# A planned one-core graph kernel: fewer early sums, one batch fewer kept on chip, one more left for the last stage, and both ends rearranged

## The chip, the core and the metric

The kernel runs as one program on one core of one Trainium2 chip. The metric is the device time of one execution in microseconds (us), lower is better. The core has a matrix engine (PE in the profile, its weight loads PEld), a vector engine (DVE), a scalar engine (ACT), a general engine (POOL) and a queue engine (SP) that issues most transfers. Engines run beside each other, each takes its own instructions in their written order, and they wait for each other through semaphores. A result of the PE goes to one of eight banks of PSUM and is read from there by ACT or DVE.

## The reference

There are 32 graphs ("batches") of 512 nodes with 128 features, `x` of (32, 512, 128), and a symmetric 0/1 adjacency `adj` of (32, 512, 512). Four layers follow each other, each of them a residual on a normalised input. Cut to what is computed:

```python
def layer0(x, mask, Wv, bv, Wk, bk, Wq, bq):          # masked attention
    v, q, k = (relu(x @ W.T + b) for W, b in ((Wv, bv), (Wq, bq), (Wk, bk)))
    s = q @ k.T
    h = clip(s * mask, 0, 9e13) - 9e15 * (1 - mask)
    return softmax(h, axis=2) @ v

def layer1(x, A, conv_w, conv_b, w_ih, w_hh, b_ih, b_hh):
    A_norm = d_inv[:, :, None] * (A + I) * d_inv[:, None, :]      # d: row sums of A + I
    dyn = conv1d(x[:, -128:, :], conv_w, padding=1) + conv_b      # the last 128 nodes
    lw = lstm(dyn, w_ih, w_hh, b_ih, b_hh)                        # 128 steps, all 32 batches side by side
    return sigmoid((A_norm @ x) @ lw)

def layer2(nodes, A, params):                          # four sublayers, fed by skips
    for i in range(4):
        src = l2norm(A, 2) @ (nodes @ ws + bs)
        dst = l2norm(A, 1).T @ (nodes @ wd + bd)
        nodes = tanh(concat(src, nodes @ wn + bn, dst) @ wu + bu)
    return nodes

def layer3(x, A, W, bias, a):
    g = A @ (x @ W.T) + bias
    return where(g >= 0, g, a * g)

for layer in (layer0, layer1, layer2, layer3):
    x = x + layer(relu(layernorm(x)), adj)
```

## The kernel before, in words

The function `symmetric` is what runs; `general` is a fallback that is entered only when a flag, computed from the data, says so. In its last lines every engine loads that flag (`counted`, `read`) and branches on it, so the branch is the last thing of each engine.

**Recorded, then planned.** The kernel's helpers (`PE`, `ACT`, `DVE`, `POOL`, `DMA`) don't emit instructions. They record operations with an assumed duration, a rank and the buffers they read and write. `Plan.run` then sets all of them in time by a list schedule with those assumed durations, and emits each engine's instructions in the order of the planned starts. So a constant that only the planner reads (`SWITCH`, `HOLD`, `LANDED`, `STORED`, `PATIENCE`, `LEAD`, `FIRST_GAPS`) costs nothing by itself on the chip, and yet can reorder all engines. `SWITCH` is what the planner assumes for the PE's change between whole-array and quarter-array matmuls; `LANDED` and `STORED` are how long after its issue a transfer is assumed to be complete; `PATIENCE` is by how much a long operation may run over the moment at which the LSTM's next operation is expected.

**Four stages.** `pass_1` takes a batch's keys, values and last 128 nodes through layer 0, far enough for the LSTM's input. It stores keys, hidden features and values to DRAM (`f_dkq`, `f_dv`), except for the batches in `RESIDENT`, which come last in pass 1 and keep theirs on chip. `lstm` then runs the 128 steps, each a chain PE `f_z` (line 1303), ACT `f_th` (1329), DVE `f_cu` and `f_th` (1335, 1336), ACT `f_tcn` (1343), DVE `f_h` and the turned copy into `f_seq` (1348, 1349), which the next step's `f_z` needs as its weights. Beside it, `pass_2` computes the other 384 nodes of layer 0: `f_pq` (1399), four score blocks `f_s` (1409), and `f_po` (1415), all quarter-array matmuls. Their order between two LSTM steps is the planner's. `rest` then does layers 1 to 3 of a batch.

**Which batch does what where.** For batches in `EARLY` (0 to 23) pass 2 also computes layer 1's sums beside the LSTM (`f_pg`, eight whole-array matmuls through `aggregate`, line 1538), stores them (`f_dgT`) and `rest` loads them again. The next two (`NEXT`, 24 and 25) and two more (`FIRST`, 26 and 27) go first through `rest`; `FIRST` keep their adjacency on chip from pass 2. The last `LATE` batches (28 to 31) have the lowest priority in pass 2, load only 384 columns of the adjacency there, and compute their sums in `rest`.

**The ends.** At the start ACT's queue loads the attention weights, the column biases and a row bias (`load_beside`), then ACT loads its function table; SP loads `x` and `adj` of the first batches; the PE runs 20 `warm_up` matmuls on zeros until the first `x` is normalised. At the end the last batch is split into two halves; 16 more warm-ups fill the PE's waits; DVE's `f_x` (1709), ACT's `f_neg` (1713) and DVE's `f_x` (1714) form the result of each half, which SP and ACT store. The recorded order of the flag's load is "after the last stores' issue".

Of the kernel before, what the change touches and what calls it, by code (L numbers as in the profile page):

```python
# [521 lines left out]
class Plan:  # L522
# [11 lines left out]
    SLACK = {"PE": 0.25, "ACT": 0.05, "DVE": 0.05, "POOL": 0.05, "SP": 0.05}  # L534


    SWITCH = (0.28, 0.1)
    HOLD = 0.15
    AHEAD = 264
    FETCH = 4.8  # L540
# [72 lines left out]
    def run(self, tc, queues):  # L613
# [15 lines left out]
        for o in ops:  # L629
            if o.rank >= self.last:  # L630
                k, sub = divmod(o.rank - self.last, 10)
                if sub == 2:
                    apart.add(o)
                soon = self.soon if k < 2 and sub < 2 else 0.0
                first = self.lead if sub == 4 else 0.0
                o.rank = self.last - soon + 12 * k - 9 * max(0, k - 28) + 200.0 - first - (min(behind[o], 60) if sub == 5 else behind[o] + (70 if sub == 2 else 0.0))
        self.left = sum(o.rank < self.URGENT for o in ops)
        free = {}
# [155 lines left out]
def symmetric(ctx, tc, x, adj, weights, cols, rows, lstm_b, prelu_a, out, fail):  # L794
# [16 lines left out]
    L = NT - 1  # L811
    NR = N - P
    MANY = 512 // (4 * B)
    LATE = 4
    FIRST = [B - LATE - 2 + k for k in range(2)]
    EARLY = range(24)
    NEXT = [len(EARLY), len(EARLY) + 1]
    FOLD_AT = (2, 3, 4, 5)
    SD_AT = 65
    BOUNCED = 8  # L820
    Q_FIRST = range(0)
    RESIDENT = range(3)
    FIRST_GAPS = (2.0, 2.8, 3.0, 3.5)
    LEAD = 0.0
    Q_AT = 3
    MOVED = range(2, B - 2)
    TURN = 32
    T_STEP = 0.22
    SOON = 9_950.0
    LANDED = 3.3  # L830
    STORED = 3.0
    PATIENCE = 1.3
    plan_rest = 30_000
    assert D == P and N == 512

# [14 lines left out]
    def flat(ap):  # L850
        return ap.rearrange("p a b -> p (a b)")
# [26 lines left out]
    def t_dve(n):  # L878
        return 0.145 + n * 0.00088
# [7 lines left out]
    def ACT(rank, t, fn, r=(), w=(), **k):  # L887
        return plan.op({"ACT": (t, fn)}, rank, r, w, **k)

    def DVE(rank, t, fn, r=(), w=(), **k):  # L890
        return plan.op({"DVE": (t, fn)}, rank, r, w, **k)
# [4 lines left out]
    def DMA(rank, kb, fn, r=(), w=(), **k):  # L896
        return plan.op({"SP": (max(0.45, t_dma(kb)), fn)}, rank, r, w, gap=k.pop("gap", 2.0), **k)
# [6 lines left out]
    def evict(rank, n, dst, src, r, w, relu=False, scale=None):  # L904

        def act():
            nc.scalar.activation(dst(), src(), AF.Relu if relu else AF.Copy, **({} if scale is None else {"scale": scale}))

        def dve():
            if relu:  # L910
                nc.vector.tensor_scalar_max(dst(), src(), 0.0)
            elif scale is not None:
                nc.vector.tensor_scalar_mul(dst(), src(), scale)
            else:
                nc.vector.tensor_copy(dst(), src())

        slow = 0.0 if scale is None else 0.2
        return plan.op({"ACT": (t_act(n) + slow, act), "DVE": (t_dve(n), dve)}, rank, r, w)
# [34 lines left out]
    def load(rank, kb, dst, src):  # L953
        c = plan.fixed(dst)
        DMA(rank, kb, lambda: nc.sync.dma_start(dst, src), [], [c])
        return c

    def load_beside(dst, src, c, gap):
        return ACT(HEAD, 0.45, lambda: nc.scalar.dma_start(dst, src), [], [c], gap=gap)

    w_att, w_cols = plan.fixed(w), plan.fixed(colb)
    load_beside(w[:, :W_CONV, :], weights[:, :W_CONV, :], w_att, 3.5)
    load_beside(colb, cols, w_cols, 3.0)
    load_beside(brow[:, BR_V, :], rows[R_V].partition_broadcast(P), (biases, BR_V), 3.0)
    ACT(HEAD, 1.5, lambda: nc.scalar.activation(table, neg_half[:, 0, 0:1], AF.Exp))
    w_conv = load(HEAD + 12, 192, w[:, W_CONV:W_IH, :], weights[:, W_CONV:W_IH, :])
    w_crow = load(HEAD + 12, 64, conv_row, rows[R_CONV].partition_broadcast(P))
    w_lb = new("n0", (P, 8, TURN), "f_lb")
    for j in range(P // TURN):
        part = bass.ts(j, TURN)  # L970
# [12 lines left out]
        c = bank(name)  # L983
        PE(rank, t, lambda: nc.tensor.matmul(c.t, marks[:, :P], marks, start=True, stop=True), [], [c], after=after)

    for k in range(20):
        warm_up(HEAD, 0.43 if k < 8 else 0.216, f"f_warm_{k}")

    def bias_row(rank, k, row, r):
# [174 lines left out]
    def pass_1(b, pos):  # L1164
# [1 line left out]
        xc = new("x", (P, NT, P), f"f_x_{b}")  # L1166
        n = 2 if pos == 0 else NT
        for at in range(0, NT, n):
            DMA(R, 64 * n, lambda at=at: nc.sync.dma_start(xc.t[:, at : at + n, :], x[b].rearrange("(t p) d -> p t d", p=P)[:, at : at + n, :]), [],
                [(xc, t) for t in range(at, at + n)] if pos == 0 else [xc], gap=FIRST_GAPS[pos] if pos < len(FIRST_GAPS) else 3.5)  # L1170
        al = new("n1", (P, NT, P), f"f_al_{b}")
        DMA(R + 11, 256, lambda: nc.sync.dma_start(al.t, adj[b, :, NR:].rearrange("(t p) i -> p t i", p=P)), [], [al])
# [383 lines left out]
    def rest(b, turn, lw_after):  # L1556
# [117 lines left out]
                turn_tiles(p4.t, lambda t: nodes[4].t[:, bass.ts(t, P)])  # L1674
            end4 = PE(R, 4 * T_TR, back, [nodes[4]], [p4])
        if turn == B - 1:
            for k in range(2 * BUFS["mm"]):
                warm_up(R - 4, 0.216, f"f_warm_{k}_{b}", [end4])
        DVE(R, t_dve(N), lambda: nc.vector.scalar_tensor_tensor(flat(xc.t), p4_t(), 0.5, flat(xc.t), OP.add, OP.add),
            [p4], [xc])  # L1680
# [7 lines left out]
        for at in range(0, NT, n) if n < NT else ():  # L1688
            cols = slice(at * P, (at + n) * P)
            p3a = bank(f"f_pg3_{b}_{at}", (P, n * P), whole=False)  # L1690
            for k in range(2):
                for j in range(NT):
                    agg3 = PE(R, t_r(n * P), lambda p3a=p3a, cols=cols, k=k, j=j: nc.tensor.matmul(
                        p3a.t, hp.t[:, j, k, :], ar.t[:, j, cols], start=(k == 0 and j == 0), stop=(k == 1 and j == NT - 1)),
                        [(hp, (k, j)), ar], [p3a], count=2)
            evict(R, n * P, lambda cols=cols: g3.t[:, cols], lambda p3a=p3a: p3a.t, [p3a], [(g3, at)])
        neg = new("xn", (P, NT, P), f"f_neg_{b}")

        for at in range(0, NT, n):
            mine = [(xc, t) for t in range(at, at + n)]  # L1700
            p3 = bank(f"f_p3_{b}_{at}", (P, n, P), whole=n == NT, filled=True)
            fill(R, lambda p3=p3: p3.t, bias(BR_3, n), [(biases, BR_3)], p3, [agg3] if n == NT else [end4])

            def fc_mm(at=at, p3=p3):
                for j in range(n):
                    nc.tensor.matmul(p3.t[:, j, :], g3.t[:, bass.ts(at + j, P)], w_fc, start=False, stop=True, skip_group_check=True)  # L1706
            PE(R, n * t_mm(P), fc_mm, [(g3, at), w_last], [p3])
            part = slice(at, at + n)
            DVE(R, t_dve(n * P), lambda p3=p3, part=part: nc.vector.scalar_tensor_tensor(
                flat(xc.t[:, part, :]), flat(p3.t), 0.0, flat(xc.t[:, part, :]), OP.max, OP.add), [p3], mine)  # L1710

            def finish(turned=(), split=(), at=at, p3=p3, part=part, mine=mine):
                ACT(R, t_act(n * P), lambda: nc.scalar.activation(neg.t[:, part, :], p3.t, AF.Relu, scale=-1.0), [p3], [(neg, at)], after=turned)
                DVE(R, 0.15 + 0.125 * n, lambda: nc.vector.scalar_tensor_tensor(
                    flat(xc.t[:, part, :]), flat(neg.t[:, part, :]), minus_alpha, flat(xc.t[:, part, :]), OP.mult, OP.add),
                    [(neg, at), w_alpha], mine, after=split)

                def store():
                    return (nc.scalar if at else nc.sync).dma_start(out[b].rearrange("(t p) d -> p t d", p=P)[:, part, :], xc.t[:, part, :])
                return ACT(R, 0.5, store, mine, [], gap=0.0) if at else DMA(R, 64 * n, store, mine, [], gap=0.0)  # L1720
            if turn in (B - 3, B - 2):
                put_off.append(finish)
            else:
                stored = finish()
            if turn == B - 1:
                late.append(stored)


    ok = const.tile([P, B, NT], FP, name="f_ok")
# [3 lines left out]
    def counted():  # L1733
        R = 30_000 + (B - 1) * 10
        bads = plan.fixed(bad)

        def exponentials():
            nc.vector.tensor_single_scalar(ok, rinv, 1e-30, OP.is_ge)
            nc.vector.scalar_tensor_tensor(flat(ok), flat(rinv), 2.0, flat(ok), OP.is_le, OP.mult)
            nc.vector.tensor_reduce(bad[:, 0:1], flat(ok), AX.X, OP.add)  # L1740
            nc.vector.tensor_scalar(bad[:, 0:1], bad[:, 0:1], -1.0, float(B * NT), OP.mult, OP.add)
        DVE(R, 0.9, exponentials, [], [bads], after=sum_ops)

        def places():
            nc.vector.tensor_reduce(bad[:, 1:2], viol, AX.X, OP.add)
            nc.vector.tensor_add(bad[:, 0:1], bad[:, 0:1], bad[:, 1:2])
        DVE(R, 0.4, places, [], [bads], after=differ_ops)
        pf = bank("f_pbad", (P, 2), whole=False)
        PE(R, 0.2, lambda: nc.tensor.matmul(pf.t[:, 0:1], ones, bad[:, 0:1], start=True, stop=True), [bads], [pf])
        said = DVE(R, 0.15, lambda: nc.vector.tensor_scalar_min(fail, pf.t[:, 0:1], 1.0), [pf], [bads])  # L1750

        def read():
            flag[0] = nc.values_load(fail[0:1, 0:1], min_val=0, max_val=1,
                                     skip_runtime_bounds_check_because="it is only compared with zero")
        PE(R + 4, 0.1, read, [], [], after=[said] + late)

    sum_ops, differ_ops, late, differs = [], [], [], [0]
    for i, at in enumerate(FOLD_AT):
# [102 lines left out]
```

## Time and profile before

| what | value |
|---|---|
| median of 3 runs | 1277.08 us |
| lowest and highest | 1275.09 and 1279.99 us |
| the profiled execution's own time | 1275.34 us |
| its span, first to last instruction | 1273.4 us |
| TensorE clock granted, mean | 0.998 |
| PE busy | 1255.8 us, 99% of the span |
| DVE busy | 985.9 us, 77% |
| ACT busy | 837.8 us, 66% |
| traffic | 232.02 MB, mean 182 GB/s |

Busy shares are means over stages, and each stage has limits of its own. The end of a matmul is modelled in the record, and matmuls overlap, so a PE that counts as busy can still be stalled; what a stretch of the PE is worth is better read from the distance between starts. "Idle before" gives how long an engine had nothing running ahead of an instruction, and after the arrow what ended that. An execution's time is some 2 us more than its span, for what lies ahead of the first and behind the last instruction.

### The profile page before, as it was taken

The page shows a single profiled execution, that of the slowest core. Times are in us where ns is not written, and L with a number is a line of the kernel's source. Part 1 is how long each engine was busy: PE and PEld are TensorE (multiplying, and loading weights), DVE is VectorE, ACT ScalarE, POOL GpSimd, SP SyncE. Part 2 cuts the span into 40 slices and gives each one's busy share as a digit, 9 for nine tenths or more (in the row PEclk, how much of TensorE's full clock was granted, in tenths as well). Part 3 has the DMA queues.
Part 4 walks back from the last instruction along what each step waited for, and adds up shares of the span by engine and source line. Part 5 has one row for each costly group of instructions (what it writes and reads, how often), then busy time and mean ns, then how long its engine had stood idle before and what let it go on. Part 6 is the DMA issues. An engine that isn't in the chain of part 4 may idle for free.

```text
span 1273.4 us, 33089 instructions
## 1 busy us (share of the span) xinstructions
PE 1255.8 (99%) x12074; PEld 970.9 (76%) x12075; DVE 985.9 (77%) x3275; ACT 837.8 (66%) x2102; POOL 400.7 (31%) x734
## 2 busy tenths in 40 slices
PE   9999999999999999999999999999999999999997
PEld 7988876666666767777778787787787877877775
DVE  7899869989899889775677677676776776787755
ACT  4667677778777667774576676666766766675433
POOL 3556533324233135331223233232242232332001
PEclk9999999999999999999999999999999999999999
DMA  8888887778986797876476677777777777482211
GB/s 270 255 274 277 275 270 233 213 226 272 277 259 214 213 251 210 174 175 160 83 178 156 155 173 160 153 174 152 175 154 151 175 157 153 89 174 59 50 33 37
DMA packets 313052, 232.02 MB, mean 182 GB/s; under 512 B 151601, under 2 KB 258481, under 8 KB 312881
## 3 DMA queue, kind: packets, MB, share of 16 engines
q1 hardware_dynamic: 295280, 212.65, 61.5%
q0 software_dynamic: 16896, 16.78, 8.5%
q8 instruction: 97, 1.59, 0.5%
q14 instruction: 75, 0.61, 0.2%
q10 hardware_dynamic: 704, 0.40, 0.1%
HBM read 135.73 MB, written 62.58 MB: 156 GB/s over the span
## 4 chain that ended last, share of the span: by engine, by line
PE 86%; DVE 6%; POOL 2%; ACT 2%; DMA 2%; issue 1%; SPq 0%; ACTq 0%; DVEq 0%
PE f_pa L1538 18%; PE f_py L1647 15%; PE f_pa L1658 15%; PE f_pg L1538 8%; PE f_po L1415 5%; PE f_z L1303 4%; PE f_s L1409 4%; PE f_pol L1251 2%; PE f_pk L1177 2%; PE f_p L1706 2%; PE f_sl L1241 2%; PE f_pv L1219 2%; PE f_pl L1612 2%; PE f_pd L1276 2%; PE f_pq L1399 1%; DVE f_e L1413 1%
## 5 line engine op out<-in xcount | busy, mean ns | idle before, releaser
L1538 PE MATMUL f_pa<-f_ar,f_y 128*128 128x512 f32 x1024 | 298.0, 428 | 0.2 <-ACT f_y L1501 0.2
L1538 PEld LDWEIGHTS f_pa<-f_ar,f_y 128*128 128x128 f32 x1024 | 189.3, 188 | 73.1 <-issue 38.7
L1647 PE MATMUL f_py<-f_wf,f_n 128*128 128x128 f32 x1280 | 173.7, 275 | 0.0
L1647 PEld LDWEIGHTS f_py<-f_wf,f_n 128*128 128x128 f32 x1280 | 165.0, 191 | 10.1 <-issue 2.9
L1662 ACT ACTIVATE f_n<-f_pa,f_bcol 128x512 f32<-128x512 f32 x128 | 88.3, 690 | 101.9 <-PE f_pa L1658 99.0
L1658 PE MATMUL f_pa<-f_n,f_wf 128*128 128x512 f32 x320 | 152.7, 593 | 0.1
L1456 ACT ACTIVATE f_ar<-f_a 128x512 fp32r<-128x512 f32 x224 | 138.7, 622 | 4.1 <-PE f_pg L1538 2.4
L1463 POOL DMA_DIRECT2D f_das<-f_ar x32 | 27.1, 846 | 360.2 <-ACT f_ar L1456 338.1
L1501 ACT CAST f_y<-f_py 128x512 fp32r<-128x512 f32 x128 | 75.3, 589 | 72.1 <-PE f_py L1647 65.5
L1502 DVE TENSOR_TENSOR f_y<-f_py,f_y 128x512 fp32r<-128x512 f32 x128 | 87.7, 687 | 34.9 <-ACT f_y L1501 33.4
L1654 DVE TENSOR_TENSOR f_pa<-f_pa,f_inv 128x512 f32<-128x512 f32 x128 | 86.9, 694 | 28.0 <-PE f_pa L1538 27.9
L1415 PE MATMUL f_po<-f_v,f_e 128*32 128x129 f32 x3072 | 108.0, 273 | 0.4 <-DVE f_e L1413 0.2
L1415 PEld LDWEIGHTS f_po<-f_v,f_e 128*32 128x32 f32 x3072 | 90.9, 110 | 21.1 <-issue 16.6
L1658 PEld LDWEIGHTS f_pa<-f_n,f_wf 128*128 128x128 f32 x320 | 57.9, 190 | 47.0 <-issue 42.6
L1409 PE MATMUL f_s<-f_q,f_k 128*32 128x384 f32 x928 | 92.0, 486 | 0.2 <-issue 0.2
L1303 PE MATMUL f_z<-f_w,f_seq 128*32 128x128 f32 x2040 | 83.4, 276 | 5.2 <-DVE f_seq L1349 2.3
L1303 PEld LDWEIGHTS f_z<-f_w,f_seq 128*32 128x32 f32 x2040 | 53.0, 109 | 45.1 <-ACT f_e L1412 10.0
L1132 DVE COPY f_hl_d<-f_n 128x1024 uint16<-128x1024 uint16 x27 | 18.7, 694 | 88.0 <-ACT f_n L1662 88.0
L1472 DVE SCALAR_TENSOR_TENSOR f_aT<-f_a,f_aT 128x1024 bf16<-128x1024 f32 (+1 forms) x68 | 76.3, 1152 | 0.5 <-DMA f_aT<-f_das 0.5
L1647 PE MATMUL f_py<-f_wf,f_T_c 128*128 128x128 f32 x448 | 72.8, 275 | 0.0
L1538 PE MATMUL f_pg<-f_ar,f_xp_d 128*128 128x512 f32 x248 | 71.9, 413 | 0.0
L1538 PE MATMUL f_pg<-f_ar,f_xp_c 128*128 128x512 f32 x256 | 68.4, 407 | 0.6 <-ACT f_xp_c L1509 0.4
(213 smaller groups left out, 2755.1 us busy)
## 6 DMA issues: line engine op xcount, KB each, us to landing
f_a<-in_adj_dram SPq DMA_DIRECT2D x112, 256.0 KB
f_a<-in_adj_dram SPq DMA_DIRECT2D x28, 1024.0 KB
f_das<-f_ar POOLq DMA_DIRECT2D x32, 512.0 KB, 4.8
f_dkq<-f_kh SPq DMA_DIRECT2D x29, 448.0 KB
f_al<-in_adj_dram SPq DMA_DIRECT2D x32, 256.0 KB
f_inv<-f_ddi SPq DMA_DIRECT2D x32, 256.0 KB
f_x<-in_x_dram SPq DMA_DIRECT2D x31, 256.0 KB
out_dram<-f_x SPq DMA_DIRECT2D x31, 256.0 KB
```

The costliest lines, as they stand in the source:

```text
L1303: nc.tensor.matmul(z.t[part, k, :, :], h, w[:, m : m + 4, part], start=False, stop=True, skip_group_check=True)
L1409: PE(R, t_mm(NR), lambda s=s, j=j: quarters(lambda p: nc.tensor.matmul(s.t[p], keys_of()[:, j * P + p.start : j * P + p.stop], q_of(), sta ...
L1415: PE(R, t_mm(P), lambda e=e, t=t, j=j: quarters(lambda p: nc.tensor.matmul(po.t[p, t, :], e.t[:, t * P + p.start : t * P + p.stop], v.t[:, ...
L1456: ACT(rank, 0.62, lambda t=t: nc.scalar.activation(ar.t[:, t, :], a.t[:, t, :], AF.Square, accum_out=deg.t[:, t : t + 1]), [(a, t)], [(ar, ...
L1472: nc.vector.scalar_tensor_tensor(flat(aT.t[:, n * k : n * (k + 1), :]), flat(a.t[:, n * k : n * (k + 1), :]), 1.0, flat(aT.t[:, n * k : n ...
L1501: ACT(rank, t_act(N), lambda: nc.scalar.copy(parts.t[:, :, 0, :], src.t), [src], [(parts, 0)])
L1502: DVE(rank, t_dve(N), lambda: nc.vector.tensor_sub(parts.t[:, :, 1, :], src.t, f32(parts.t[:, :, 0, :])), [src, (parts, 0)], [(parts, 1)])
L1538: nc.tensor.matmul(pg.t, parts.t[:, j, k, :], ar.t[:, j, :], start=(k == 0 and j == 0), stop=(k == 1 and j == NT - 1))
L1647: nc.tensor.matmul(py.t[:, j, :], nodes[n].t[:, bass.ts(j, P)], wf[:, W_F[i] + c, 0, :], start=False, stop=(c == nch - 1), skip_group_chec ...
L1654: before = DVE(R, t_dve(N), lambda pa=pa: nc.vector.tensor_mul(pa.t, pa.t, inv_row.t), [inv_row], [pa])
L1658: nc.tensor.matmul(pa.t, wf[:, W_F[i] + c, 1, :], nodes[n].t, start=False, stop=(c == nch - 1), skip_group_check=True)
L1662: ACT(R, 0.57, lambda pa=pa, n=n, i=i: nc.scalar.activation(n.t, pa.t, AF.Tanh, bias=bcol[:, i : i + 1]), [pa], [n])
```

## The change

Nothing is computed differently. Constants that choose the batches change: `EARLY` is 0 to 22, and with `LATE` at 5 `NEXT` becomes 23 and 24, `FIRST` 25 and 26, and five batches (27 to 31) come late; `RESIDENT` is 0 and 1. Constants that only the planner reads change. At the start ACT's queue takes the small biases first, then its function table, then the weights; the first three batches' `x` come ahead of the rest, and three warm-ups go. At the end 16 warm-ups become 7 and 3, DVE's first step of a result moves into `finish` (so that for batches whose `finish` is put off it is put off too), and the flag is loaded after the last evictions instead of after the stores.

```diff
-    SWITCH = (0.28, 0.1)
+    SWITCH = (0.25, 0.12)
...
-                first = self.lead if sub == 4 else 0.0
+                first = self.lead if sub == 4 else 60.0 if sub == 3 else 0.0
...
-    LATE = 4
+    LATE = 5
     FIRST = [B - LATE - 2 + k for k in range(2)]
-    EARLY = range(24)
+    EARLY = range(23)
     NEXT = [len(EARLY), len(EARLY) + 1]
...
-    RESIDENT = range(3)
-    FIRST_GAPS = (2.0, 2.8, 3.0, 3.5)
-    LEAD = 0.0
+    RESIDENT = range(2)
+    FIRST_GAPS = (2.0, 2.5, 3.0, 3.5)
+    LEAD = 8.0
...
-    LANDED = 3.3
-    STORED = 3.0
-    PATIENCE = 1.3
+    LANDED = 3.8
+    STORED = 3.5
+    PATIENCE = 1.5
...
-    load_beside(w[:, :W_CONV, :], weights[:, :W_CONV, :], w_att, 3.5)
     load_beside(colb, cols, w_cols, 3.0)
+    ACT(HEAD, 1.5, lambda: nc.scalar.activation(table, neg_half[:, 0, 0:1], AF.Exp))
+    load_beside(w[:, :W_CONV, :], weights[:, :W_CONV, :], w_att, 3.0)
     load_beside(brow[:, BR_V, :], rows[R_V].partition_broadcast(P), (biases, BR_V), 3.0)
-    ACT(HEAD, 1.5, lambda: nc.scalar.activation(table, neg_half[:, 0, 0:1], AF.Exp))
-    w_conv = load(HEAD + 12, 192, w[:, W_CONV:W_IH, :], weights[:, W_CONV:W_IH, :])
-    w_crow = load(HEAD + 12, 64, conv_row, rows[R_CONV].partition_broadcast(P))
+    w_conv = load(HEAD + 22, 192, w[:, W_CONV:W_IH, :], weights[:, W_CONV:W_IH, :])
+    w_crow = load(HEAD + 22, 64, conv_row, rows[R_CONV].partition_broadcast(P))
...
-    for k in range(20):
+    for k in range(17):
         warm_up(HEAD, 0.43 if k < 8 else 0.216, f"f_warm_{k}")
...
-            DMA(R, 64 * n, lambda at=at: nc.sync.dma_start(xc.t[:, at : at + n, :], ...
+            DMA(R if pos > 2 else HEAD + pos, 64 * n, lambda at=at: nc.sync.dma_start(xc.t[:, at : at + n, :], ...
...
         if turn == B - 1:
-            for k in range(2 * BUFS["mm"]):
+            for k in range(7):
                 warm_up(R - 4, 0.216, f"f_warm_{k}_{b}", [end4])
...
-            evict(R, n * P, lambda cols=cols: g3.t[:, cols], lambda p3a=p3a: p3a.t, [p3a], [(g3, at)])
+            late.append(evict(R, n * P, lambda cols=cols: g3.t[:, cols], lambda p3a=p3a: p3a.t, [p3a], [(g3, at)]))
+            for k in range(3 if at else 0):
+                warm_up(R - 4, 0.216, f"f_warm_{k}_{at}_{b}", [agg3])
...
-            DVE(R, t_dve(n * P), lambda p3=p3, part=part: nc.vector.scalar_tensor_tensor(
-                flat(xc.t[:, part, :]), flat(p3.t), 0.0, flat(xc.t[:, part, :]), OP.max, OP.add), [p3], mine)
-
             def finish(turned=(), split=(), at=at, p3=p3, part=part, mine=mine):
+                DVE(R, t_dve(n * P), lambda: nc.vector.scalar_tensor_tensor(
+                    flat(xc.t[:, part, :]), flat(p3.t), 0.0, flat(xc.t[:, part, :]), OP.max, OP.add), [p3], mine, after=split if turn == B - 2 else ())
...
-                stored = finish()
-            if turn == B - 1:
-                late.append(stored)
+                finish()
...
-        PE(R + 4, 0.1, read, [], [], after=[said] + late)
+        PE(R + 3, 0.1, read, [], [], after=[said] + late)
```

More of the change, by code (lines that the diff above doesn't have):

```diff
@@ L1168, in pass_1 @@
         for at in range(0, NT, n):
-            DMA(R, 64 * n, lambda at=at: nc.sync.dma_start(xc.t[:, at : at + n, :], x[b].rearrange("(t p) d -> p t d", p=P)[:, at : at + n, :]), [],
+            DMA(R if pos > 2 else HEAD + pos, 64 * n, lambda at=at: nc.sync.dma_start(xc.t[:, at : at + n, :], x[b].rearrange("(t p) d -> p t d", p=P)[:, at : at + n, :]), [],
                 [(xc, t) for t in range(at, at + n)] if pos == 0 else [xc], gap=FIRST_GAPS[pos] if pos < len(FIRST_GAPS) else 3.5)
```

## The prediction

> **What bounds the kernel now.** I read the page first, then stretches by stage, then the matrix engine in order of time inside the LSTM, then both ends.
>
> ```profile
> span 1273.4 us, 33089 instructions
> PE 1255.8 (99%) x12074; PEld 970.9 (76%) x12075; DVE 985.9 (77%) x3275; ACT 837.8 (66%) x2102; POOL 400.7 (31%) x734
> ```
>
> The PE is busy nearly everywhere, so time moves only with the PE's work, or with stalls that its record hides. The stretches (span, then busy time and instructions of PE, PEld, DVE, ACT, POOL, granted clock, DMA share, GB/s) show where those can be:
>
> ```profile
> 0.00:13.00 13.00, 10.66 (x49) 6.05 (x50) 7.75 (x41) 3.61 (x8) 3.53 (x15) 1.00 0.81 231
> 13.00:185.00 172.00, 170.91 (x1378) 150.52 (x1380) 148.23 (x648) 116.97 (x246) 92.85 (x233) 1.00 0.84 272
> 185.00:493.00 308.00, 302.28 (x6389) 211.71 (x6385) 272.91 (x1132) 229.20 (x816) 97.27 (x178) 1.00 0.82 243
> 493.00:520.00 27.00, 26.44 (x256) 21.16 (x247) 24.62 (x86) 19.39 (x50) 10.96 (x16) 1.00 0.82 152
> 520.00:1190.00 670.00, 669.58 (x3621) 523.65 (x3620) 485.13 (x1249) 438.12 (x929) 189.96 (x284) 1.00 0.69 150
> ```
>
> From 520 to 1190 us the PE loses 0.42 us in 670: nothing to win. Beside the LSTM (185 to 493) it loses 5.7 us openly, with DVE at 89%. The PE in order of time (start, length, line, tiles, records) shows what is hidden:
>
> ```profile
> 302.09 0.64 PE L1303 MATMUL f_z<-f_w,f_seq 128*32 128x128 f32 x16
> 302.56 0.83 PE L1399 MATMUL f_pq<-f_h,f_w 128*32 128x384 f32 x8
> 303.20 1.28 PE L1415 MATMUL f_po<-f_v,f_e 128*32 128x129 f32 x40
> 304.30 0.62 PE L1303 MATMUL f_z<-f_w,f_seq 128*32 128x128 f32 x16
> 306.51 0.65 PE L1303 MATMUL f_z<-f_w,f_seq 128*32 128x128 f32 x16
> 307.08 2.11 PE L1538 MATMUL f_pg<-f_ar,f_xp_c 128*128 128x512 f32 x8
> 309.12 0.64 PE L1303 MATMUL f_z<-f_w,f_seq 128*32 128x128 f32 x16
> ```
>
> One step is from one `f_z` to the next. Start to start a record costs 27 ns for `f_z` and `f_po` (1.10 us / 40), 80 ns for `f_pq` and `f_s`, 227 ns for a sum `f_pg`. So the first step holds 0.43 + 0.64 + 1.10 = 2.17 us of work and lasts 2.21; the step with an early sum holds 0.43 + 1.82 = 2.25 and lasts 2.61. Done for all 127 steps in the program's order: 276.2 us of work in 306 us from first to last step, so 30 us are lost, all of the kernel's real slack but for the ends. Steps with under 2.0 us of work still last 2.15 to 2.2: the chain PE, ACT, DVE, ACT, DVE, PE is a floor of about 2.17.
>
> At the end, the chain of waits:
>
> ```profile
> 1262.27 1.18 PE f_pg L1693 x10
> 1263.45 1.09 PE f_warm L984 x5
> 1264.55 0.46 PE f_p L1706 x4
> 1265.03 0.42 DVE f_x L1709
> 1265.90 0.93 DVE f_x L1714 x2
> ```
>
> Five warm-ups stand on the chain, though the evictions that `f_p` needs end at 1263.91. At the start, warm-ups run from 1.19 and the first real matmul (the transposes, 7.45) follows them directly, while the first half of its input was ready at 6.56; and DVE later waits 1.17 us for the third batch's `f_x` (10.70).
>
> **What the Trainium skill says.** "TensorE: Matmul & The Clock Gate", section "What's actually happening": the PE's clock halves after an idle window of about 3.4 us. The trace agrees in kind: warm-ups start 0.43 us apart up to 5.0 us and 0.216 after. With 17 and 10 warm-ups no gap of that length opens before the last matmul, so I charge nothing. "TensorEngine Tiling (Array Packing)", "Key Properties": changing the tiling mode drains the PE; the step with the sum above lost 0.36 us across its two changes. "PSUM — Partial Sum Buffer", "PSUM bank collisions raise a hardware error": two engines may not read one bank at once; hence `f_neg` waits for `f_x` in the trace (1265.03 + 0.42, then ACT at 1265.49), and that order matters at the end.
>
> **The change part by part.**
>
> *Work of the PE.* In the two built programs the matmuls differ by 9 warm-ups (36 to 27) and one transpose `f_plw` (12 to 13; 0.11 us). Pass 2 and the sums are only moved. In the third batch's scores the keys come from another buffer; the same matmuls.
>
> *Head.* Three warm-ups at 0.216 us: 0.65, if `x` allows; the first half was ready 0.68 before the PE took it, the second at 7.60, and that must come sooner too. The first `x` no longer shares the transfers with 192 KB of weights, and the third `x` is issued fourth instead of seventh, so a part of the 1.17 us wait goes too. Against it, the weights are issued after the table load (about 2.7 instead of 0.74) and might arrive at 6 to 7.7; `f_pk` needed them at 8.30, now about 7.65. I take -1.0, bounds -2.0 and +0.3.
>
> *Residents 3 to 2.* Batch 2 now stores 448 + 258 KB and loads 448 + 258 + 192 KB: two more stores and four more loads on SP, 1.6 MB, at 243 to 272 GB/s 6.2 us of transfers. They are covered by the idle 16 to 18% of the DMA engines in those 493 us. In the built order its loads stand directly behind the adjacency of batch 1. Cost 0; upper bound under the rivals.
>
> *Early sums 24 to 23.* Four squares (622 ns) and one store and load of 256 KB less beside the LSTM; in the last stage one diagonal subtraction more (0.7 us, DVE at 72% there). Hidden. The sum, 1.82 us, moves to a stage without loss and takes its 0.36 with it: -0.4.
>
> *LSTM stage.* The program's order has 45 steps with less than 2.0 us of work, 32 before, and more long ones. With the floor, the sum over 127 steps of max(2.17, work + 0.1) is 296.3 before and 295.4 after, a gain of 0.9, while 3.3 us of work have left the stage (276.2 to 272.9) and must be done outside. Net +2.4; with 0.06 or 0.15 in place of 0.1, +2.9 or +1.9. With the sum, +2.0. The later landings and the patience show in this order only; mode changes in the stage fall from 54 to 52.
>
> *Entry and exit of the LSTM.* Before, two convolutions (`f_pd`) stood ahead of `f_z` with 0.8 us of `f_po` between; after, one, and 0.45 us: the last addition into `f_seq` (378 ns plus two crossings) is then late by some 0.4. At the exit `f_po` of batch 31 covered the first layers of `FIRST`; now pass 2 is done earlier. Five links of batches 25 and 26 have only 0.86 to 0.91 us of other work where ACT's copy (589 ns) or DVE's product (694 ns) plus crossings need about 1.0 to 1.15. The trace shows such a link, 0.44 us wide, stalling 0.24. Together +0.7. Sum +1.1, bounds 0 and +2.
>
> *End.* Six warm-ups fewer at 0.216 are 1.3 of PE work; two of the five on the chain go for certain (0.4), and the last batch's transposes stand 0.9 earlier in order. Loading the flag before the stores takes 0.5 from ACT's and SP's way to the branch. Against it, the second half's `f_x` now waits for its `f_neg`, which puts ACT's last store some 0.45 later. I take -0.8, bounds -1.8 and +0.5.
>
> Sum: -1.0 + 2.0 + 1.1 - 0.8 = +1.3 us. On the profiled execution that is 1275.3 to 1276.6; that execution is 1.7 below the median of the runs (its span 1.9 below its time), so for the median 1277.1 to 1278.4.
>
> **Rivals.**
>
> *The floor gives way.* With less between two steps, DVE and ACT reach the chain's instructions sooner, and the stage loses no more than now: the +2.4 vanishes. -1.0 - 0.4 + 0.7 - 0.8 = -1.5, about 1275.5. For it: DVE is 89% busy and takes the chain's operations in its own order. Against: in the records 57% of the steps already start within 0.15 us of the turned `h`.
>
> *The ends are hidden.* The weights or `x` bind at the start, the last store's landing at the end (issued 1266.87, the program ends 6.5 us later): only the middle's +3.1 remains, 1280.
>
> *A late batch 2 (slower).* Its keys come from DRAM just as the LSTM begins. If they land later than its `f_pq`, the PE stands in order with the LSTM's steps behind it. All of the 6.2 us exposed on top of +1.3 makes 1284.6; it decides once batch 2's loads take over 6 us from issue. Against: transfers ended almost no wait in that stage.
>
> *More gained than I see.* Both ends at their bounds and the loss beside the LSTM smaller by 3: 1270.5.
>
> **How the numbers follow.** Forecast 1278.4: 0.42, own range 1276 to 1280. Floor gives way 0.24; ends hidden 0.16; late batch 2 0.12; more gained 0.06. 0.5% is 6.4 us, about what a measurement of this kernel tells from no change: faster means under 1270.7, slower over 1283.5. Only the last two cases cross that: slower 0.13, faster 0.06, same 0.81. The range 1272 to 1285 takes in all but the outer cases.
>
> **What would show it.** Right: from the first to the last `f_z` about 305 us, with more steps near 2.2; transposes at about 6.6; one or two more idle gaps of 0.1 to 0.3 behind `f_py` of the first two batches; the last `f_p` about 1 us nearer to its `f_pg`. Wrong: a wait of `f_pq` or `f_s` for batch 2's landing; steps under 2.1 us; the stretch after the exit no longer without loss; or a changed distance between the last `f_x` and the end.

## The result and the profile after

The changed kernel takes 1280.15 us (median of 22 runs, 1277.03 to 1282.94) against 1276.72 us for the kernel before (22 runs). The ratio is 1.0023, interval 1.0015 to 1.0032: 2.9 us slower, well inside the half per cent that counts as no change. The forecast was 1278.4, so the total is near, inside the range of 1272 to 1285 and just above the narrower one of 1276 to 1280. It is near by luck: two terms were wrong by 4.8 and 3.7 us in opposite directions, and that is what the experiments show.

The page of the changed kernel, span and busy time (instructions behind the x):

```profile
span 1275.7 us, 33054 instructions
PE 1254.1 (98%) x12067; PEld 969.7 (76%) x12067; DVE 982.9 (77%) x3269; ACT 840.8 (66%) x2102; POOL 397.4 (31%) x732
```

Its stretches, as before: span, busy time and instructions of PE, PEld, DVE, ACT and POOL, granted clock, DMA share, GB/s.

```profile
0.00:13.00 13.00, 9.07 (x35) 4.34 (x36) 6.86 (x37) 3.47 (x7) 3.52 (x15) 1.00 0.73 227
13.00:185.00 172.00, 170.92 (x1383) 151.20 (x1386) 148.05 (x649) 115.35 (x238) 93.27 (x231) 1.00 0.85 272
185.00:493.00 308.00, 299.80 (x6334) 208.59 (x6330) 273.49 (x1130) 226.16 (x803) 90.33 (x172) 1.00 0.81 246
493.00:520.00 27.00, 26.24 (x298) 21.60 (x290) 24.68 (x100) 19.34 (x52) 15.60 (x25) 1.00 0.76 155
520.00:1190.00 670.00, 669.70 (x3620) 524.65 (x3619) 480.49 (x1231) 445.53 (x947) 188.46 (x282) 1.00 0.67 150
```

In the first 13 us the PE is busy 9.07 us, where it was 10.66: 0.65 of that is the three warm-ups, the rest is new waiting. Beside the LSTM it is busy 299.80 instead of 302.28. From 520 us on there is still nothing to lose.

The head, DVE in order of time (start, length, line, what it writes and reads, and in brackets how long it was idle and what ended that):

```profile
3.08 0.49 DVE L1081 BATCH_NORM_STATS2 f_st_a<-f_x 128x6 f32<-128x128 f32 x2 [1.80 <-DMA f_x<-in_x_dram]
...
5.41 0.29 DVE L1081 BATCH_NORM_STATS2 f_st_a<-f_x 128x6 f32<-128x128 f32 x1 [1.62 <-DMA f_x<-in_x_dram]
...
8.18 0.48 DVE L1081 BATCH_NORM_STATS2 f_st_a<-f_x 128x6 f32<-128x128 f32 x2 [1.79 <-DMA f_x<-in_x_dram]
8.58 0.59 DVE L1192 TENSOR_SCALAR f_xn_a<-f_x,f_mv_a,f_rs_a 128x128 f32<-128x128 f32 x2
```

The first half of the first `x` does land 1.1 us earlier (3.08 instead of 4.18). But the pair of statistics at 8.18 belongs to the second batch: DVE waits 1.79 us for that batch's `x`, and the first batch's normalisation `f_xn_a` stands behind it in DVE's order. In the kernel before, the normalisation of the first half came first (5.96). The PE at the same place:

```profile
5.67 1.24 PE L984 MATMUL f_warm<-f_marks 128*128 128x512 bf16 x5
9.05 0.50 PE L1198 MATMUL f_xt_a<-f_ident,f_xn_a 128*128 128x128 f32 x2 [2.14 <-DVE f_xn_a L1192]
```

The first transposes start at 9.05 instead of 7.45, after 2.14 us of nothing. Beside the LSTM, the PE in order of time, a short step and one with an early sum:

```profile
297.92 0.64 PE L1303 MATMUL f_z<-f_w,f_seq 128*32 128x128 f32 x16
298.38 1.95 PE L1415 MATMUL f_po<-f_v,f_e 128*32 128x129 f32 x64
300.24 0.64 PE L1303 MATMUL f_z<-f_w,f_seq 128*32 128x128 f32 x16
300.68 0.43 PE L1415 MATMUL f_po<-f_v,f_e 128*32 128x129 f32 x8
301.04 2.11 PE L1538 MATMUL f_pg<-f_ar,f_xp_c 128*128 128x512 f32 x8
303.07 0.65 PE L1303 MATMUL f_z<-f_w,f_seq 128*32 128x128 f32 x16
```

The same prices hold: 2.32 us for 0.43 + 1.73 of work, 2.83 for 0.43 + 0.22 + 1.82. And the end of the chain of waits:

```profile
1265.40 0.90 PE f_p L1708 x8
...
1266.33 0.70 DVE f_x L1712
...
1267.06 0.48 ACT f_neg L1714
...
1267.55 0.39 ACT f_g L907
...
1267.98 0.73 PE f_p L1708 x4
...
1268.73 0.44 DVE f_x L1712
```

No warm-up stands directly ahead of the last `f_p` any more. Batch 30's result has taken their place: with its first step put off too, its `f_neg` stands on ACT ahead of the eviction `f_g` that the last `f_p` needs.

### The profile page after: what moved, and what is told of

It reads as the page before. It is cut to its first block, busy times and chain, and to the rows that moved or that the text cites. A ratio compares the mean times of both kernels' runs of the same rounds, so it can differ in the third digit from the quotient of the medians.

```text
span 1275.7 us, 33054 instructions
## 1 busy us (share of the span) xinstructions
PE 1254.1 (98%) x12067; PEld 969.7 (76%) x12067; DVE 982.9 (77%) x3269; ACT 840.8 (66%) x2102; POOL 397.4 (31%) x732
## 4 chain that ended last, share of the span: by engine, by line
PE 90%; DVE 5%; ACT 3%; POOL 1%; issue 1%; DMA 1%; SPq 0%; ACTq 0%; DVEq 0%; POOLq 0%
PE f_pa L1538 18%; PE f_py L1647 15%; PE f_pa L1658 15%; PE f_pg L1538 9%; PE f_s L1409 5%; PE f_po L1415 5%; PE f_z L1303 5%; PE f_pol L1251 2%; PE f_sl L1241 2%; PE f_pv L1219 2%; PE f_pk L1177 2%; PE f_p L1708 2%; PE f_pl L1612 2%; PE f_pd L1276 2%; PE f_pq L1399 2%; PE f_xt_a L902 1%
## 5 line engine op out<-in xcount | busy, mean ns | idle before, releaser
L1409 PE MATMUL f_s<-f_q,f_k 128*32 128x384 f32 x960 | 96.7, 486 | 2.4 <-issue 2.4
L1412 ACT ACTIVATE f_e<-f_s 128x384 f32<-128x384 f32 x128 | 61.2, 484 | 12.2 <-PE f_s L1409 8.0
```

The costliest lines, as they stand in the source:

```text
L1409: PE(R, t_mm(NR), lambda s=s, j=j: quarters(lambda p: nc.tensor.matmul(s.t[p], keys_of()[:, j * P + p.start : j * P + p.stop], q_of(), sta ...
```

## The experiments

In the time of each run "ratio" is against the kernel before, with its interval; one thousandth is 1.28 us. The ratio is the number to go by, since the medians of the kernel before differ by a microsecond between series (1276.45, 1276.61 and 1277.50). Profiled stretches are distances between starts on the PE. In the head, `f_xt_a` are the first batch's transposes, `f_pk` and `f_pql` its keys and queries; `f_py` and `f_pa` are the matmuls of layer 2's sublayers, so the stretch from the first `f_py` to the last `f_pa` is nearly all of the last stage, and `f_p` is layer 3's last matmul.

**1. The head of before in the changed kernel.** From the LSTM on, every engine's order stays that of the changed kernel.

```diff
-    FIRST_GAPS = (2.0, 2.5, 3.0, 3.5)      # and ACT's load order, the ranks of x and of the weights
+    FIRST_GAPS = (2.0, 2.8, 3.0, 3.5)
-    for k in range(17):
+    for k in range(20):
```

> The changed kernel with its head alone undone (load order, 20 warm-ups, ranks of x, assumed gaps of x); every engine's order from the LSTM on stays that of the changed kernel. Theory A (the head is where the forecast failed: DVE has the statistics of the second batch's x ahead of the first batch's normalisation and waits for that x): first transposes back from 9.05 to about 7.45 us, first f_z from 187.1 to 185.5 to 186.0, first-to-last f_z unchanged at about 307.6, end of the span 1.1 to 1.6 us earlier than the changed kernel's 1275.7. Rival R1 (the early stage is bound by its transfers and absorbs the delay): transposes at 7.45 but first f_z within 0.3 of 187.1, end within 0.3. Rival R2 (all of the loss is beside the LSTM): no gain at the end.

1276.55 us, ratio 0.9997 (0.9987 to 1.0008): the whole loss is gone, so the head accounts for it, and the rival that puts it all beside the LSTM falls. First transposes at 7.07, first `f_z` at 184.83 instead of 187.11, even earlier than expected. R1, absorption by the early stage, falls too. The profile itself came out long (span 1277.8 where 1274.1 to 1274.6 was expected), although the LSTM's order is that of the changed kernel: its first-to-last `f_z` took 312.4 us instead of 307.5, a miss of the expectation. The longest of its PE's waits, around 430 us (us in total, times, longest):

```profile
PE f_s L1409 <- issue: 2.6, 1, 2.6
```

"Issue" is a wait for nothing that this view shows; the last section says what it goes with. The same is in the profile of the changed kernel, at 470 us (its waits from 185 to 497 us):

```profile
PE f_z L1303 <- DVE f_seq L1349: 3.4, 11, 0.7
PE f_s L1409 <- issue: 2.4, 2, 2.1
```

Its counterpart in the kernel before came to 0.2. So one execution of an order can hold 2 us that the next one does not, and two profiles can't be compared to 2 us beside the LSTM. From here on I use means over all executions of one order.

**2. One constant of the head taken back.**

```diff
-    FIRST_GAPS = (2.0, 2.5, 3.0, 3.5)
+    FIRST_GAPS = (2.0, 2.8, 3.0, 3.5)
```

> The changed kernel with one planner constant of its head taken back: the assumed gaps of the first x are 2.0, 2.8, 3.0, 3.5 as before. DVE then has the first batch's normalisation ahead of the second batch's statistics; loads, ranks and the 17 warm-ups stay those of the change. Theory A: first transposes at 7.2 to 7.6 instead of 9.05, because no engine waits for the second x any more. Rival R3 (the first x or the attention weights, now issued later on ACT's queue, land too late): transposes still after 8.3, or f_pk waits for f_w. The plan beside the LSTM changes with it; from the fit of steps (a step lasts the longer of 2.24 us and its work + 0.10, + 0.29 if a sum is in it) the 126 steps should take 305.5 us against 302.7 in the changed kernel, so the end may not come earlier.

1282.03 us, ratio 1.0044 (1.0027 to 1.0061). The first two transposes came at 7.20, as expected, but only the first half: two statistics of the second batch still stood ahead of the second half's normalisation, so the other two transposes came at 8.76 and `f_pk` at 9.09. The first `f_z` stayed at 186.81, and beside the LSTM the new plan took 309.6 us from first to last `f_z` against 307.5. The single constant can't be judged by the time, since it replans everything behind it.

**3. The end alone**, on the kernel before: the lines of the diff with `first = self.lead` and `LEAD`, and all from `range(7)` on.

> The kernel before with only the end of the change (7 and 3 warm-ups, finish with its first step, flag loaded after the last evictions, and the ranks that go with it). Orders ahead of the last batch stay those of before. Theory A: 1.0 to 1.4 us faster than before (span about 1272.2), last store's issue to the end of the span 4.7 instead of 6.5 us, the last p3 to the last f_x 0.5 longer. Rival (the ends are hidden, the last landing sets the end whatever is ahead of it): within 0.3 of before.

1275.68 us, ratio 0.9994 (0.9984 to 1.0004), so -0.8 with an interval of -2.0 to +0.5. The last `f_pa` to the end of the span took 20.28 us instead of 21.36; the last store's issue to the end 4.6 instead of 6.5; and the last `f_pa` to the last `f_p` 0.5 longer. These three are as the theory had it; the time falls short of its 1.0 to 1.4, and the interval doesn't exclude the rival's 0.3.

**4. The head alone**, on the kernel before.

> The kernel before with only the head of the change. Theory A: the same DVE order as in the changed kernel, transposes at about 9.05 instead of 7.45, first f_z 0.7 to 1.6 later, LSTM unchanged at 306.2, end 0.7 to 1.6 us later than before. Rival R1 (absorbed by transfers of the early stage): end within 0.3 of before. The forecast on record: 1.0 us earlier.

1280.87 us, ratio 1.0030 (1.0021 to 1.0038): +3.8, the largest part of the change, and the forecast of -1.0 for it is refuted. It is also more than twice what theory A had (0.7 to 1.6). Transposes at 8.93, first `f_z` at 186.80.

**5. The normalisation first, in the changed kernel.** Loads, ranks, warm-ups and all other engines' orders stay; only DVE's order of six instructions in the head moves.

```diff
         order.sort(key=lambda o: (o.start, o.no))
+        end = max(order.index(o) for o in self.normed)               # the first batch's f_xn_a
+        held = [o for o in order[:end] if o in self.stats[10_010]]    # the second batch's f_st_a
+        order[:end + 1] = [o for o in order[:end + 1] if o not in held] + held
```

> The changed kernel with one thing altered after the planning: DVE's statistics of the second batch's x are emitted behind the first batch's four normalisations instead of among them. All other engines' orders are those of the changed kernel. Theory A (DVE's in-order wait for the second x is the cost of the head): first transposes from 9.05 to 7.2 to 7.6, f_pk from 10.1 to about 8.3, first f_z 0.9 to 1.7 earlier than 187.1, time about 1278 to 1279 (1280.2 for the changed kernel). Rival R3 (the loads land too late whatever DVE does): transposes or f_pk still after 9. Rival R4 (DVE is then late with f_kh, behind the same wait): transposes early, f_pql still near 11.8 and first f_z unchanged.

1276.86 us, ratio 1.0006 (0.9996 to 1.0016), below the expected 1278 to 1279. DVE in order of time:

```profile
5.66 1.28 DVE L1196 TENSOR_SCALAR f_xn_a<-f_x,f_mv_a,f_rs_a 128x128 f32<-128x128 f32 x4 [0.21 <-POOL f_rs_a L1095]
7.88 0.87 DVE L1085 BATCH_NORM_STATS2 f_st_a<-f_x 128x6 f32<-128x128 f32 x4 [0.93 <-DMA f_x<-in_x_dram]
```

All four normalisations now end at 6.94, and the second `x` still lands at 7.88. The PE:

```profile
7.46 0.60 PE L1202 MATMUL f_xt_a<-f_ident,f_xn_a 128*128 128x128 f32 x4
8.32 1.13 PE L1181 MATMUL f_pk<-f_kh,f_w 128*128 128x256 f32 x4 [0.26 <-ACT f_kh L911]
10.50 0.49 PE L1181 MATMUL f_pql<-f_kh,f_w 128*128 128x128 f32 x2 [1.05 <-DVE f_kh L1184]
```

Transposes and `f_pk` are where they were before the change, with the new loads and 17 warm-ups: R3 falls. R4 is right in part: DVE's `f_kh` is late behind the same second `x`, and `f_pql` waits 1.05 us for it. First `f_z` 185.76, 1.35 earlier than in the first profile of the changed kernel. This run shows most directly that DVE's order is needed for the head's loss, since it changes nothing else and takes most of the loss away. Whether the order alone is enough is the question of the next run.

**6. The planner's gap alone**, on the kernel before, with its loads:

```diff
-    FIRST_GAPS = (2.0, 2.8, 3.0, 3.5)
+    FIRST_GAPS = (2.0, 2.5, 3.0, 3.5)
```

> The kernel before with a single planner constant changed, the assumed gap of the second x from 2.8 to 2.5; only DVE's first 40 instructions change their order (statistics of the second x ahead of the first normalisation), loads stay those of before, every other order too. Theory A (it is the order together with the later landing of the second x): before, that x had landed by 6.61, so DVE waits 0.3 to 0.6 at most, transposes at 7.5 to 8.0, time within 0.8 us of before. Rival (the order alone costs it): transposes at about 9.

1276.93 us, ratio 1.0003 (0.9995 to 1.0012). In time theory A holds, in the profile its rival does. DVE, in order of time:

```profile
7.88 0.49 DVE L1081 BATCH_NORM_STATS2 f_st_a<-f_x 128x6 f32<-128x128 f32 x2 [2.29 <-DMA f_x<-in_x_dram]
8.29 0.59 DVE L1192 TENSOR_SCALAR f_xn_a<-f_x,f_mv_a,f_rs_a 128x128 f32<-128x128 f32 x2
```

The second `x` lands at 7.88 with the loads of before, too. In five more profiles with those loads it had landed by 6.61, 6.90, 7.19, 7.26 and 7.89, with those of the change at 7.88 to 8.24. So the 6.61 of the profile that the forecast was made from was the earliest of six. On average the second `x` came 0.8 us later with the loads of the change (8.05 against 7.29), so they have a part in the wait. The kernel before can suffer from it too: its DVE has the statistics of the second `x` between the two halves of the first normalisation, and in experiment 3, where that `x` landed at 7.89, the second pair of transposes came at 8.77 and `f_pk` at 9.10. In this run the first transposes came at 8.76, but the first `f_z` only 0.9 later than the mean with the old head (184.9). The order alone, with the old loads and 20 warm-ups, is therefore not enough for the +3.8.

**7. The middle alone**, on the kernel before.

```diff
-    LATE = 4
+    LATE = 5
-    EARLY = range(24)
+    EARLY = range(23)
-    RESIDENT = range(3)
+    RESIDENT = range(2)      # and SWITCH, LANDED, STORED, PATIENCE
```

> The kernel before with only the middle of the change: batches (23 early sums, two residents, five late) and the planner's SWITCH, LANDED, STORED and PATIENCE; both ends stay. The forecast on record: +3.1 us. Theory B, from the first runs (head of before with this middle and the new end took 1276.55, the new end alone 1275.68): +0.4 to +1.3, because the stalls that differ between two executions of one and the same order (up to 4 us) hide what the floor of the LSTM step costs. Rival (the middle gains, the end gives it away): -0.5 or less.

1276.47 us, ratio 0.9995 (0.9984 to 1.0006): -0.6, interval -2.0 to +0.8, short of theory B's +0.4 to +1.3 and right at the start of the rival's. The forecast's +3.1 is excluded.

**8. The flag alone**, on the kernel before, with `finish` and the 16 warm-ups as they were.

```diff
-                first = self.lead if sub == 4 else 0.0
+                first = self.lead if sub == 4 else 60.0 if sub == 3 else 0.0
...
+            late.append(evict(...))
-                stored = finish()
-            if turn == B - 1:
-                late.append(stored)
+                finish()
-        PE(R + 4, 0.1, read, [], [], after=[said] + late)
+        PE(R + 3, 0.1, read, [], [], after=[said] + late)
```

> The kernel before with only the flag's load moved ahead of the last stores (after the evictions of the last sum); finish, the 16 warm-ups and all other orders stay. Theory A (the last store's landing does not set the end alone; the branch behind it does): last store's issue to the end of the span from 6.5 to about 4.7 us, time 1.5 to 1.9 us faster than before, which would be more than the whole new end gives, since the moved first step of finish costs 0.5 and puts batch 30's result on the chain. Rival (the store is issued later or the landing takes as long): within 0.4 of before.

1276.1 us, ratio 0.9994 (0.9985 to 1.0003). The last instructions that touch the output, in order of time (the span ends at 1275.28):

```profile
1269.71 0.48 DVE L1714 SCALAR_TENSOR_TENSOR f_x<-f_neg,f_minus_alpha,f_x 128x256 f32<-128x256 f32 x1
1270.22 0.41 ACTq L1719 DMA_DIRECT2D out_dram<-f_x  x1
```

From the last issue to the end 5.06 us instead of 6.54; from the last `f_pa` to the end 20.29 instead of 21.36. That is 1.1, less than the 1.5 to 1.9 expected, and as much as the whole new end gives, so that the rest of the end's edits pays for itself and no more. In the time the -0.8 has an interval of -1.9 to +0.4, which does not exclude the rival. One more order changed with the flag: DVE now finishes the first half's result before it begins the second's. From its first `f_x` on a half to the last issue it takes 2.24 us instead of 1.84, and so the flag itself gave 1.5 and that order took 0.4 of it back.

**9. The changed kernel again.**

> The changed kernel once more, beside the others on one chip. The runs give its head 3.3 to 3.8 us, the profiled executions only 1.3 to 2.4. Theory A1 (the second x lands at different times in different executions, and the first profiles were lucky ones): transposes in this profile anywhere from 8.5 to 10.5, time 1279 to 1281. Rival (a part of the 3.3 is not in the head): transposes again at 9.05 and stalls elsewhere that kernels with the old head don't show.

1279.76 us, ratio 1.0017 (1.0005 to 1.0028). Transposes at 9.11: that is in A1's range, but hardly other than the 9.05 and 8.93 of the first two profiles, so nothing speaks for luck in their landings, as A1 had it. But the first `f_z` came at 187.88, and the stretches say why:

```profile
5.00:9.00 4.00, 2.69 (x9) 0.90 (x7) 1.42 (x10) 0.00 (x0) 1.38 (x2) 1.00 0.94 298
9.00:11.00 2.00, 1.67 (x6) 1.09 (x7) 2.00 (x13) 0.77 (x2) 0.26 (x1) 0.76 0.79 233
11.00:13.50 2.50, 2.50 (x11) 2.05 (x11) 2.16 (x9) 1.24 (x3) 0.75 (x1) 0.51 0.76 263
```

In this execution the granted clock (third number from the end) fell to one half behind the wait. `f_pk` took 1.92 us instead of 1.34, and by 13.5 us some 0.7 us were lost against the first profile of the same kernel.

**10. and 11. The two loads apart**, both on the kernel before with the gap of 2.5 and 20 warm-ups: first the ranks of the first three `x` and of the convolution weights, then ACT's load order.

```diff
+            DMA(R if pos > 2 else HEAD + pos, 64 * n, ...       # 10
+    ACT(HEAD, 1.5, ...table...) ahead of the weights' load      # 11
```

> The kernel before with the ranks of the first three x and of the convolution weights and with the gap of 2.5, so DVE's order of the changed head and the third x issued fourth on SP; ACT's load order and the 20 warm-ups stay. Theory A2 (the third x shares the transfers with the second one, which DVE waits for): most of the head's +3.8, that is +2 to +4 us. Rival (ACT's later weights are what delays the second x): +0.3 as with the gap alone.

> The kernel before with ACT's new load order (column biases, table, weights, row bias) and the gap of 2.5, so DVE has the second batch's statistics first; SP's issue order and the 20 warm-ups stay. Theory A2: +0.3 to +1 us, as with the gap alone (+0.3). Rival (ACT's later weights delay the second x): +2 to +4 us.

Ratios 0.9999 (0.9988 to 1.0010) and 1.0001 (0.9991 to 1.0012): neither costs what the whole head does, and both the A2 of the first and the rival of the second, which had +2 to +4 us, fall. In the profiles transposes came at 8.90 and 9.22, the second `x` at 8.02 and 8.34, first `f_z` at 186.96 and 186.34. So the wait was there, and 20 warm-ups had left 0.4 and 1.1 us of idle time ahead of the transposes instead of 1.4 to 2.2. The profiles give these two heads +1.4 to +2.1 at the first `f_z`, the times about nothing; experiment 4 is the other way round (+1.9 and +3.8). That three warm-ups fewer matter through the clock is a guess from experiment 9 that no run tried: the whole head with 20 warm-ups was not run.

The mean granted clock of every execution is on record, and it supports the guess in part. In the changed kernel it was 0.997 or less in 22 of 35 executions (those of experiment 9 counted in), with the same middle and end and the head of before (experiment 1) in none of 14. The means are 0.9973 and 0.9986; on 1276 us the difference is worth 1.6 us of the clock, an estimate, and one fall as in experiment 9, 3.4 us at one half, is worth 1.7. In the head alone (experiment 4) eight executions had 0.999, the profiled one among them, and took 1278.8 us on average; the fourteen below took 1281.3. So the profiles may show the head cheaper than it mostly is. But the mean does not say where in an execution the clock fell, and for experiment 4 it is only 0.0003 lower than before, worth 0.4 us. What lies between the +1.9 of its profile and the +3.8 of its times stays open.

**12. A mended version**: the kernel before with the flag moved (8), ACT's load order, 17 warm-ups, and the normalisations first (5).

> A version meant to beat both: the kernel before with the flag's load moved, ACT's new load order, 17 warm-ups (three left out after the planning, so that no order changes) and the second batch's statistics behind the first batch's normalisations; batches, planner constants and SP's issue order as before. Theory A: head 0.3 to 0.8 earlier, since all four normalisations wait for the first x alone, end 0.5 to 1 earlier: 1274.8 to 1275.8 against 1276.6, interval below 1. Rival (the warm-ups' end or the weights bind the first transposes, and the end's gain is within what the runs can tell): within 0.4 of before.

1276.15 us, ratio 0.9986 (0.9978 to 0.9993): 1.8 us faster than the kernel before, at the far end of what was expected, and so faster than both. The PE in the head:

```profile
6.83 1.02 PE L1202 MATMUL f_xt_a<-f_ident,f_xn_a 128*128 128x128 f32 x4
7.68 1.34 PE L1181 MATMUL f_pk<-f_kh,f_w 128*128 128x256 f32 x4
10.76 0.49 PE L1181 MATMUL f_pql<-f_kh,f_w 128*128 128x128 f32 x2 [1.74 <-DVE f_kh L1184]
```

Transposes 0.6 earlier than before, as the forecast had wanted of the head. What was gained there is lost again at `f_pql`, which waits 1.74 us for a DVE that waits for the second `x`: that is the next thing to mend. Its first `f_z` at 185.33 is no earlier than with the old head. Its profiled span was long (1277.1; 309.9 us from first to last `f_z`), so that the gain rests on the times, and in the profile on the end alone (20.0 us from the last `f_pa`, 21.4 before).

## Why the prediction was right, and where it was wrong

The parts alone, from the times (ratio less one, times 1276.6) and from the profiles (means over all executions of the same order: the first `f_z` 184.9 with the old head in five, 187.3 with the changed one in three; the last `f_pa` to the end 21.1 with the old end in six, 20.4 with the new one in five; experiment 2, with its own plan, is left out):

| part | forecast | time | profiles |
|---|---|---|---|
| head | -1.0 | +3.8 (+2.7 to +4.9) | +2.4 |
| middle: LSTM, entry, exit, residents | +3.1 | -0.6 (-2.0 to +0.8) | -0.2 |
| end | -0.8 | -0.8 (-2.0 to +0.5) | -0.7 |
| sum | +1.3 | +2.4; all together +2.9 | +1.5 |

**The head is the step that failed**, in sign, and outside its bounds of -2.0 to +0.3. The forecast reckoned with landings and warm-ups, and took for granted that DVE goes on as before. It does not: with the second `x` assumed 0.3 us earlier, the planner puts that batch's statistics ahead of the first normalisation, DVE waits for a landing at 8.2, and the PE waits for DVE. That order is needed for the loss: put right with all else kept, the changed kernel's 1.0023 becomes 1.0006 (experiment 5). It is not enough for it: experiments 6, 10 and 11 have the same order and the transposes at 8.8 to 9.2, and their times are within 0.4 us of before. They have 20 warm-ups; what leaving out three adds is argued from the granted clock and not shown. The planned order of the changed program was to be had without a run, and the forecast read it for the LSTM and not for the first twenty instructions of DVE. Two smaller slips: the second half of the first `x` came no sooner (5.41, 4.72 and 4.50 in three profiles, by 4.80 before), so the hoped-for 7.60, for which DVE's order counted as well, would not have moved much; and the weights were issued at 1.32, not 2.7, because ACT's queue issues while the table loads. That one cost nothing.

**The LSTM stage.** The floor is there: steps with under 2.0 us of work took 2.2 us on average before and after (one 2.06 us stall left out), 32 of them before and 44 after. The term +2.0 was mis-sized by its other half. From first to last `f_z` the order of before took 307.6 us in the mean of eight executions, that of the changed kernel 309.2 in five, with 1.6 us less of the PE's work in the program; so the stage seems to lose about 3.2, where the forecast had 2.4. The ranges overlap (305.4 to 309.9 and 307.4 to 312.4), so this is a hint and not a measurement. (The 3.3 us that it let leave the stage were counted wrong: 1.7 of them lie in the first step.) But the work that leaves it was taken as paid in full elsewhere, and the profiles do not show that. With 1.3 us more work ahead of the first `f_z`, that came 0.4 earlier (two profiles with this middle and the old head against three); with 0.4 more at the exit, that took 0.1 longer; and from the first `f_py` to the last `f_pa`, with equal work, 744.8 instead of 746.2 (744.4 to 745.0 in five executions, 745.3 to 748.5 in eight). Why the last stage gained a microsecond is open: no run was made for it, and the PE shows as busy there in both.

**Entry and exit** at +1.1 did not show either: exit +0.1, and ahead of the first `f_z` a gain, though of few profiles. What the times exclude is the middle's +3.1 as a whole. **Residents** at 0 hold: beside the LSTM only one weight load of the PE waited for a landing of keys, 0.2 us. **The end** at -0.8 is near, but not by its terms: the second half's `f_x` cost 0.4 (0.45 estimated), the flag gained 1.5 (0.5 estimated), and batch 30's `f_neg` on ACT, which the forecast did not have, put the last `f_p` 0.5 later. The gain from fewer warm-ups, with a last `f_p` about 1 us nearer to its `f_pg` as its sign, did not show.

**The rivals.** "The floor gives way" was right that the middle costs nothing, for another reason; "the ends are hidden" has the nearest time (1280) and the wrong mechanism, since the end did give its 0.7. None had a head that loses. The wide range and the chance of 0.81 for no change were right because all terms are small beside 0.5%, not because the terms were.

## What to carry to other kernels

Where a planner writes an in-order queue, read the planned order of every engine around each changed constant, the first instructions above all: an assumed landing that is 0.3 us too early can put an instruction that waits ahead of one that could run. A landing that ended no wait in one profile has not been shown to be early, and here it moved by 1.3 us between executions of the same loads. Where executions of one order differ by more than the effect, take the times of the parts alone, and means over several profiles, before a term is believed.

## What the runs showed of the hardware

- One order of instructions gave 305.4 to 309.9 us from first to last `f_z` in eight executions. A good part of what differs are single stalls of the PE of up to 2.6 us that the profile calls "issue". They are not spread at random. Of the 97 transfers of queue q8, which carries instructions in blocks of 16 KB, the 57th has such a stall behind it in all five executions of the changed kernel's order, with 0.5 to 2.6 us. Shown are a line of the changed kernel's page and its PE behind that transfer, which ran from 467.80 to 468.76 us in that execution:

```profile
q8 instruction: 97, 1.59, 0.5%
470.07 1.16 PE L1409 MATMUL f_s<-f_q,f_k 128*32 128x384 f32 x10 [2.06 <-issue]
```

All 36 of these stalls beside the LSTM, in fourteen traces, ended 1.2 to 1.6 us after a transfer of q8 had ended. So the PE most likely waits there for its next instructions; no run tried to change that.
- The warm-ups' spacing fell from 0.43 to 0.216 us at 4.15 to 7.07 us in fourteen profiles, although they always began at 1.2. The Trainium skill, "TensorE: Matmul & The Clock Gate", section "What's actually happening", explains this by a free-running window of about 3.4 us. It gives the moment a scatter of 0.5 us either way, and for one kernel 6, 11 or 14 slow matmuls; here it is 2.9 us from first to last, with 7 to 14 slow warm-ups. It also has the clock fall after an idle window of about 3.4 us. In experiment 9 it fell to one half for 3.4 us with no idle gap longer than 1.43 us, so the fall needs no such gap. The forecast charged nothing because no gap of 3.4 us would open, and that was too simple; the lines that it took as agreeing show the rise alone.
- ACT's queue issued the weights' load at 1.32 us, while ACT's table load ran from 1.19 to 2.47: a load recorded behind it is not held up by it.
- How early the flag is loaded goes with how long the program lasts behind the issue of its last store, and experiment 8 shows it as the cause (5.06 us instead of 6.54): 5.8 to 6.7 us in six profiles with the load behind it, 4.6 to 5.1 in seven with the load ahead, and 6.4 in one more of these (experiment 2), which is unexplained.
